# A decoder layer on one core: where three inner values of a feed-forward half are worked out

## The chip, the cores and the metric

The kernel runs on one core of a Trainium2 chip. The metric is the device time of one execution in microseconds, and smaller is better. The profile that is read here is of one execution; the time before is the median of three runs.

## The reference

A decoder layer in float32 on four batches of 1024 tokens with 512 features. Three residual blocks follow each other, each behind a layer norm: a gated self-attention with 16 heads of 32, a cross-attention to a context of 384 features, and a feed-forward block, which is the one that matters here.

```python
x = x + attn(layernorm(x))                      # 16 heads, softmax with gates
x = x + xattn(layernorm(x), ctx)                # 16 heads, softmax(q k / sqrt(32)) v, then Wo + bo
# feed-forward: M = 64, INNER = 16
s = layernorm(x) @ Win + bin_                   # 64 values a token
h = relu(s[..., None] * W1 + b1)                # 16 inner values of each
g = einsum('btmh,mh->btm', h, W2) + b2          # summed over the 16
x = x + g @ Wout + bout
```

## The kernel before, in words

The work is cut into eight units, `order` (L336): for each of the two attentions (`ph`) the four batches. Unit 0 to 3 are the self-attention, unit 4 to 7 the cross-attention, followed by the feed-forward block of its batch. A unit has two halves of 512 queries, and a half has 32 steps: four groups of four heads (`g`), eight blocks of 128 keys (`kt`) each.

A step (`step`, L684) is written out in this order. TensorE makes the scores of one group and one block into two PSUM buffers (L574). ScalarE takes the exponential of each of the two (L579, tile `e`), which frees the buffer for the scores of the next step. VectorE adds the exponentials up (L585, L587, tile `es`). TensorE then multiplies the exponentials of the step before with the values (L601, tile `av`), and, in the self-attention and in the last unit, adds half of the heads up itself (L609, tile `sm`). In units 4 to 6 VectorE adds up both exponentials of a step, in unit 7 only one, save in the very last group. A step after a group has ended, its sums are made by TensorE (L631) and copied out by ScalarE (L618, L620, L632); they travel over DRAM, come back as reciprocals, and VectorE multiplies the group's output with them (L681).

Between the steps stands the other work: projections of the next unit, and the output projection, the norm and the feed-forward block of the half before. `beside(u, hf)` (L962) writes it out as a list of parts, each with a load; `run` (L930) hands them out to the 32 steps in proportion to their loads, in the order of the list. A part with load 0 takes no share and goes with its neighbour; `pause` is a part with a load and no work. `weave(light, items)` (L918) spreads the parts of `light` evenly among those of `items`.

The feed-forward block of a half lies in `post` (L728). `inputs` makes the 64 values a token (L841) and ScalarE copies them out (L280, tile `sT`). Then `hidden(h)` (L853), for h from 0 to 16, takes one of the 16 inner values and adds up the one before:

```python
if h < INNER:
    hid = p2.tile([P, 2 * P], F32, tag="hid", name="hid")
    nc.scalar.activation(hid, res["s"], AF.Relu, ...)                     # L858
if h == 1:
    nc.vector.tensor_scalar(res["g"], res["hid"], ...)                    # L862
elif h > 1:
    nc.vector.scalar_tensor_tensor(res["g"], res["hid"], ..., res["g"])   # L864
```

The tile `hid` has two buffers, so ScalarE's inner value h waits until VectorE has taken value h - 2. All these parts have load 0. `outputs` ends the block (L875, L881). What `some(half, k)` (L957) takes off, the first k of the 17 parts, is laid out with the half of attention in which `inputs` stands; the rest is kept in `held` and laid out with the next half. So the block of unit 6's first half, `post(6, 0)`, begins beside the second half of unit 6 (`beside(6, 1)`, L1008 to L1015) and ends beside the first half of unit 7 (`beside(7, 0)`, L966 to L977). In this last list the first six parts that are left go with a pause of ten, and all others with the 16 parts of the output projection of unit 6's second half (L972).

[...] SyncE issues the transfers.

Of the kernel before, what the change touches and what calls it, by code (L numbers as in the profile page):

```python
# [63 lines left out]
def moderate_path(tc: tile.TileContext, a: dict, out: bass.AP, flag: bass.AP):  # L64
    nc = tc.nc
    x = a["x"]
    with ExitStack() as st:
# [130 lines left out]
        def rotate(c):  # L198
            def f():
                pw = bank()  # L200
                columns(pw, rot[:, c, :], raw[0][:, c, :], start=True, stop=True)
                nc.vector.tensor_copy(raw[0][:, c, :], pw)
                if c == NC - 1:
                    nc.sync.dma_start(wout_d, raw[0])
            return [(1, f)]
# [40 lines left out]
        def load_networks(k):  # L246
            r = slice(k * M, (k + 1) * M)
            nc.gpsimd.dma_start(wout[r, :], a["ffn_Wout"])
            nc.gpsimd.dma_start(fb[r, :], a["ffb"])
            for c in range(NF):  # L250
                for w in range(3):
                    nc.gpsimd.dma_start(
                        units[k * M + c * per : k * M + (c + 1) * per, w, :],
                        a["units"].rearrange("(m h) w c -> c w m h", h=INNER)[c, w],
                    )
# [81 lines left out]
        n = len(order)  # L337
# [580 lines left out]
        def weave(light, items):  # L918

            first, second = sum(light, []), sum(items, [])  # L920
            out, done = [], 0
            for n, f in enumerate(first):
                upto = (2 * n + 1) * len(second) // (2 * len(first))
                out += second[done:upto] + [f]
                done = upto
            return [out + second[done:]]
# [14 lines left out]
        def pause(load):  # L941
            return [[(1, None)] * load]

        n = len(order)
        pres = [pre(u) for u in range(n)]

        def one(f):
            return [[(0, f)]]
# [4 lines left out]
        def ahead(u, what):  # L953

            return one(lambda: pres[u]["load"](what))

        def some(half, k):  # L957

            h, half["h"] = half["h"][:k], half["h"][k:]
            return h  # L960

        def beside(u, hf):  # L962

            last = post(u, 0) if hf else post(u - 1, 1) if u else None
            end = lambda items: weave(held[0]["h"], items) + (lambda o: o[0:1] + pause(1) + o[1:] + pause(1))(held.pop()["out"]) if held else items
            if u + 1 == n:  # L966
                h, out = held[0]["h"], last["wo"] + last["load"]
                k = min(len(h), 6)
                if hf:
                    ending.append(post(u, 1))  # L970
                    out += ending[0]["wo"]
                out += pause(2) + weave(h[0:k], pause(10)) + weave(h[k:], last["o"]) + held.pop()["out"]  # L972
                out += (ending[0]["load"] if hf else []) + weave(last["ln"], pause(5)) + last["xT"]
                out += weave(last["b"], pause(8))
                out += weave(last["tr"], pause(3)) + last["s"] + weave(some(last, 8), pause(14))
                held.append(last)
                return out  # L977
            p = pres[u + 1]
            x, ln, xT, tr, k, q, v = (p[i] for i in ("x", "ln", "xT", "tr", "k", "q", "v"))
            next_ = pres[u + 2] if u + 2 < B else None  # L980
            if u + 1 < B:
                if hf == 0:
                    if last:
                        out = x[1] + last["wo"] + last["load"] + ahead(u + 1, "v") + k[0][0:1] + p["g"][0] + k[0][1:] + p["gt"][0]
                        out += weave(ln[1], last["o"]) + xT[1] + weave(last["ln"], v[0][0:2])
                    else:
                        out = one(fold_bv) + x[1] + k[0][0:1] + [rotate(c) for c in range(NC)]
                        out += ahead(u + 1, "v") + p["g"][0] + k[0][1:2] + [[(4, fold_bv)]] + weave(ln[1], k[0][2:])
                        out += p["gt"][0] + v[0][0:1] + xT[1] + v[0][1:2]
                    return out + tr[1] + v[0][2:3] + p["g"][1] + v[0][3:] + p["gt"][1]  # L990
                if not next_:
                    out = k[1] + ahead(u + 1, "q") + last["wo"] + last["load"] + v[1] + ahead(u + 2, "k") + last["o"]
                    return out + weave(last["ln"], q[0][0:2]) + q[0][2:] + pres[u + 2]["ctx"][0] + q[1]
                out = next_["x"][0] + k[1][0:2] + last["wo"] + last["load"] + weave(next_["ln"][0], k[1][2:] + v[1])
                out += ahead(u + 1, "q") + ahead(u + 2, "k") + last["o"]
                out += weave(last["ln"], q[0][0:2]) + q[0][2:] + next_["xT"][0] + q[1][0:3] + next_["tr"][0] + q[1][3:]
                if u == 1:
                    out = one(lambda: load_networks(0)) + out + one(lambda: load_networks(1)) + one(fold_bin)
                return out
            if hf == 0:  # L1000
                out = ahead(u + 1, "v") + last["wo"] + p["ctx"][1] + end(k[0] + v[0][0:2]) + last["load"]
                out += last["o"] + weave(last["ln"], v[0][2:])
                if "s" in last:
                    out += last["xT"] + k[1][0:2] + weave(last["tr"], k[1][2:3]) + [k[1][3][0:2]] + last["s"]
                    held.append(last)
                    return out + xT[0] + weave(last["b"] + some(last, 5), [k[1][3][2:]] + v[1][0:2]) + tr[0]
                return out + k[1] + xT[0] + v[1][0:2] + tr[0]
            out = ahead(u + 1, "q") + last["wo"] + end(v[1][2:] + q[0][0:3]) + xT[1]  # L1008
            out += (ahead(u + 2, "k") if u + 2 < n else []) + last["load"] + last["o"] + tr[1]
            out += weave(last["ln"], q[0][3:] + q[1][0:1])  # L1010
            out += pres[u + 2]["ctx"][0] if u + 2 < n else []
            if "s" in last:
                out += last["xT"] + weave(last["b"], q[1][1:2]) + weave(last["tr"], q[1][2:3]) + [q[1][3][0:2]] + last["s"]
                held.append(last)
                return out + weave(some(last, 3), [q[1][3][2:]])  # L1015
            return out + q[1][1:]

        p = pres[0]
# [16 lines left out]
        for u in range(n):  # L1035
            if u == 0:
                crossing.append(True)
            for hf in range(2):
                run(attention(u, hf), beside(u, hf))
# [679 lines left out]
```

## Time and profile before

| | us |
|---|---|
| median of three runs | 2210.0 (2209.04 to 2211.79) |
| the profiled execution, its own time | 2212.44 |
| its span, first to last instruction | 2210.6 |
| TensorE busy in the span | 2174.1 (98%) |
| VectorE busy | 1562.2 (71%) |
| ScalarE busy | 1238.5 (56%) |
| one exponential (L579) | 1.022 |
| one sum of exponentials (L587) | 1.227 |
| one inner value (L858) | 0.605 |
| one product with the second weights (L864) | 0.481 |

The span is what the trace covers. PE is TensorE's matmuls, PEld its weight loads, DVE is VectorE, ACT is ScalarE, SPq is SyncE's queue. A line of the timeline gives start, length, engine, line of the kernel, operation and tiles (written, then read); "x16" says that so many instructions are put together, and the brackets give the idle time of the engine before it and who ended it. The granted clock of TensorE is 1.00 at full speed.

### The profile page before, as it was taken

Reading aid. Unit: us, or ns where it says so; the run is one execution under the profiler, and the core shown is the slowest. Engines: PE = TensorE matmul, PEld = TensorE weight load, DVE = VectorE, ACT = ScalarE, POOL = GpSimd, SP = SyncE. Lnnn points to the kernel's source line nnn. Section 1 sums busy time; section 2 is a strip of 40 time slices with the busy share of each in tenths; the row PEclk is TensorE's granted clock in tenths of the full one; section 3 lists DMA queues with packets and bytes.
Section 4 is the critical chain, followed back from the end, with each engine's and each line's share of the span. In section 5 each row is a group of like instructions: output and inputs, shape, how many; then the busy total and the mean of one; then the engine's idle time right before and its main releaser. Section 6 shows DMA issues by size and latency. Waiting matters only on the chain.

```text
span 2210.6 us, 52746 instructions
## 1 busy us (share of the span) xinstructions
PE 2174.1 (98%) x22598; PEld 547.7 (25%) x22598; DVE 1562.2 (71%) x2526; ACT 1238.5 (56%) x1489; POOL 82.0 (4%) x118
## 2 busy tenths in 40 slices
PE   8999999999999999999999999999999999999995
PEld 3322222222222222222222222222222222222222
DVE  4478675796757957577686666877787777856476
ACT  0155545555455554555556565676757566667673
POOL 1000000030300000000000000000000000000000
PEclk9999999999999999999999999999999999999998
DMA  4412123032230211211232132312233142303031
GB/s 142 132 56 63 55 98 106 24 88 66 100 106 25 85 66 55 79 37 51 60 89 89 45 87 64 101 60 65 58 98 87 60 97 64 88 12 117 21 88 40
DMA packets 153304, 161.70 MB, mean 73 GB/s; under 512 B 46202, under 2 KB 91898, under 8 KB 151908
## 3 DMA queue, kind: packets, MB, share of 16 engines
q1 hardware_dynamic: 149068, 156.14, 24.4%
q8 instruction: 179, 2.93, 0.6%
q0 software_dynamic: 2144, 0.98, 0.3%
q10 hardware_dynamic: 1848, 1.12, 0.2%
q14 instruction: 65, 0.53, 0.1%
HBM read 115.40 MB, written 42.74 MB: 72 GB/s over the span
## 4 chain that ended last, share of the span: by engine, by line
PE 92%; DVE 3%; issue 2%; DMA 2%; ACT 2%; SPq 0%; DVEq 0%; ACTq 0%
PE f L87 35%; PE s L574 24%; PE av L601 21%; PE sm L609 6%; PE sm L631 3%; DVE es L587 1%; ACT e L579 1%; PE f L875 1%; DMA xn<-rows_d 1%; DVE g L864 1%; PE f L841 1%; DMA rows_d<-r 0%; PE f L325 0%; PE f L471 0%; PE f L1025 0%
## 5 line engine op out<-in xcount | busy, mean ns | idle before, releaser
L579 ACT ACTIVATE e<-s 128x1024 f32<-128x1024 f32 x1024 | 993.7, 1022 | 713.2 <-PE s L574 518.0
L587 DVE TENSOR_TENSOR es<-es,e 128x1024 f32<-128x1024 f32 x534 | 642.3, 1227 | 255.8 <-ACT e L579 253.5
L574 PE MATMUL s<-q,k 32*64 32x512 f32 x8192 | 608.7, 614 | 4.5 <-ACT e L579 2.9
L601 PE MATMUL av<-e,v 128*32 128x512 f32 x4096 | 551.1, 604 | 0.0
L87 PE MATMUL f<-xT,w 128*32 128x512 f32 x2816 | 333.7, 592 | 0.6 <-PE f L87 0.6
L595 DVE SCALAR_TENSOR_TENSOR eg<-e,sw,eg 128x512 f32<-128x512 f32 x448 | 318.6, 747 | 2.3
L585 DVE TENSOR_TENSOR es<-e 128x1024 f32<-128x1024 f32 x89 | 106.7, 1222 | 221.0 <-ACT e L579 187.8
L574 PEld LDWEIGHTS s<-q,k 32*64 32x64 f32 x8192 | 133.1, 130 | 449.4 <-ACT e L579 243.3
L87 PE MATMUL f<-w,q 128*32 128x512 f32 x1984 | 240.5, 592 | 0.7 <-DVE q L720 0.7
L601 PEld LDWEIGHTS av<-e,v 128*32 128x32 f32 x4096 | 88.1, 108 | 404.6 <-issue 401.4
L87 PEld LDWEIGHTS f<-xT,w 128*32 128x32 f32 x2816 | 92.1, 110 | 211.3 <-issue 204.4
L609 PE MATMUL sm<-e,sw 128*2 128x512 f32 x1024 | 133.3, 592 | 0.0
L87 PE MATMUL f<-w,xT 128*32 128x512 f32 x896 | 106.0, 592 | 0.6 <-DVE q L284 0.6
L87 PEld LDWEIGHTS f<-w,q 128*32 128x32 f32 x1984 | 65.5, 110 | 150.0 <-issue 142.3
L858 ACT ACTIVATE hid<-sT,units 128x256 f32<-128x256 f32 x128 | 76.7, 605 | 31.1 <-DVE g L864 24.5
L87 PE MATMUL f<-w,ctxT 128*32 128x512 f32 x768 | 92.6, 592 | 0.0
L87 PE MATMUL f<-ctxT,w 128*32 128x512 f32 x768 | 92.3, 592 | 0.0
L778 POOL TENSOR_TENSOR r<-res,bo_bc 128x512 f32<-128x512 f32 x32 | 40.9, 1278 | 1040.5 <-DVE res L770 702.7
L631 PE MATMUL sm<-es,ones 128*1 128x512 f32 x348 | 65.8, 601 | 0.0
L864 DVE SCALAR_TENSOR_TENSOR g<-hid,units,g 128x256 f32<-128x256 f32 x120 | 57.7, 481 | 11.3 <-ACT hid L858 5.8
L770 DVE TENSOR_TENSOR res<-f,res 128x512 f32<-128x512 f32 x62 | 42.5, 686 | 17.9 <-PE f L87 8.9
L681 DVE TENSOR_TENSOR q<-both,recb 128x512 f32<-128x512 f32 x63 | 43.3, 687 | 7.5 <-DMA recb<-rec_d 7.5
(258 smaller groups left out, 1037.2 us busy)
## 6 DMA issues: line engine op xcount, KB each, us to landing
recb<-rec_d SPq DMA_DIRECT2D x252, 64.0 KB
xT<-rows_d SPq DMA_DIRECT2D x60, 256.0 KB
rows_d<-r SPq DMA_DIRECT2D x60, 256.0 KB
w<-in_xattn_Wo SPq DMA_DIRECT2D x9, 1024.0 KB
w<-wout_d SPq DMA_DIRECT2D x8, 1024.0 KB
res<-in_x SPq DMA_DIRECT2D x32, 256.0 KB
x1b_d<-r SPq DMA_DIRECT2D x32, 256.0 KB
res<-x1b_d SPq DMA_DIRECT2D x32, 256.0 KB
```

Of the source, the lines that this page charges most:

```text
L87: nc.tensor.matmul(to[r], lhsT=lhsT[:, j, :] if len(lhsT.shape) == 3 else lhsT[:, r], rhs=rhs, **flags)
L574: nc.tensor.matmul(s[m : m + 64, j, :], lhsT=k[r, g, kt * P + m : kt * P + m + 64], rhs=q[r, g, :], start=True, stop=True,)
L579: nc.scalar.activation(e, s, AF.Exp, scale=SCALE)
L585: nc.vector.tensor_tensor(me["es"][i], me["e", 0][i], es[i], ALU.add)
L587: nc.vector.tensor_tensor(me["es"][i], me["es"][i], es[i], ALU.add)
L595: nc.vector.scalar_tensor_tensor(eg, es[0][:, h, :], gate(kt), eg, ALU.mult, ALU.add)
L601: nc.tensor.matmul(av[r, :], lhsT=me["v"][:, kt, HG * g + h, :], rhs=es[h // 2][:, h % 2, :], start=(kt == 0), stop=(kt == NT - 1),)
L609: nc.tensor.matmul(sm[j * DH : j * DH + sums, :], lhsT=me["sw"][:, t, HG * g + 2 + h, :] if ph == 0 else ones, rhs=me["e", t][1][:, h, :], ...
L631: nc.tensor.matmul(sm[j * DH : j * DH + 1, :], lhsT=ones, rhs=e, start=True, stop=True)
L681: nc.vector.tensor_tensor(me["q", hf][:, g, :], both[:, 0, :], all_, ALU.mult)
L858: nc.scalar.activation(hid, res["s"], AF.Relu, bias=units[:, 1, h : h + 1], scale=units[:, 0, h : h + 1])
L864: nc.vector.scalar_tensor_tensor(res["g"], res["hid"], units[:, 2, h - 1 : h], res["g"], ALU.mult, ALU.add)
```

## The change

For unit 6 alone, no inner value of its first half's feed-forward block is laid out beside its own second half; all 17 parts go with the first half of unit 7. Units 4 and 5 keep their three.

```diff
@@ beside(u, hf) @@
             if "s" in last:
                 out += last["xT"] + weave(last["b"], q[1][1:2]) + weave(last["tr"], q[1][2:3]) + [q[1][3][0:2]] + last["s"]
                 held.append(last)
-                return out + weave(some(last, 3), [q[1][3][2:]])
+                return out + (weave(some(last, 3), [q[1][3][2:]]) if u + 2 < n else [q[1][3][2:]])
             return out + q[1][1:]
```

In the list of unit 7's first half, 17 parts instead of 14 are now spread in the same places: six with the pause of ten, eleven instead of eight with the 16 parts of the output projection. The loads of both lists are what they were, so every part with a load stays in its step.

## The prediction

> **What bounds the kernel now.** First the page: the busy times and the row of granted clock.
>
> ```profile
> span 2210.6 us, 52746 instructions
> ...
> PE 2174.1 (98%) x22598; PEld 547.7 (25%) x22598; DVE 1562.2 (71%) x2526; ACT 1238.5 (56%) x1489; POOL 82.0 (4%) x118
> ```
>
> TensorE is idle for only 36.5 us of 2210.6. Work moved between ScalarE and VectorE can therefore matter only where it makes TensorE wait or slows its clock. So I asked for TensorE's waits on ScalarE: apart from the end of the program there is one large one, 2.17 us at 1931, the join of unit 6 and unit 7, which is where the moved instructions stand. The timeline of TensorE there (start, length, work; in brackets the idle time before it and what ended it):
>
> ```profile
> 1929.01 1.11 PE L574 MATMUL s<-q,k 32*64 32x512 f32 x16
> 1930.06 1.07 PE L601 MATMUL av<-e,v 128*32 128x512 f32 x8
> 1933.30 2.89 PE L574 MATMUL s<-q,k 32*64 32x512 f32 x16 [2.17 <-ACT e L579]
> 1936.12 1.89 PE L631 MATMUL sm<-es,ones 128*1 128x512 f32 x8
> 1937.78 1.93 PE L601 MATMUL av<-e,v 128*32 128x512 f32 x8
> 1939.64 1.23 PE L574 MATMUL s<-q,k 32*64 32x512 f32 x16
> ```
>
> The reader is to see the hole, and that the same av work takes 1.07 us before it and 1.93 us after it. The busy times by stretch say why (the column after POOL is TensorE's granted clock):
>
> ```profile
> 1931.10:1933.10 2.00, 0.02 (x4) 0.00 (x0) 0.97 (x2) 1.94 (x3) 0.00 (x0) 1.00 0.02 4
> 1933.20:1939.90 6.70, 6.60 (x40) 1.36 (x48) 1.62 (x2) 4.95 (x8) 0.00 (x0) 0.50 0.00 1
> 1940.00:1946.00 6.00, 6.00 (x68) 1.34 (x56) 3.11 (x6) 4.61 (x6) 0.00 (x0) 1.00 0.03 3
> ```
>
> The hole is followed by 6.8 us at half clock. What made the hole stands in ScalarE's timeline, with VectorE's at the same time below it:
>
> ```profile
> 1928.24 0.60 ACT L858 ACTIVATE hid<-sT,units 128x256 f32<-128x256 f32 x1
> 1931.16 0.60 ACT L858 ACTIVATE hid<-sT,units 128x256 f32<-128x256 f32 x1 [2.32 <-DVE g L862]
> 1931.66 0.67 ACT L282 ACTIVATE q<-f,bqk 128x512 f32<-128x512 f32 x1
> 1932.23 1.92 ACT L579 ACTIVATE e<-s 128x1024 f32<-128x1024 f32 x2
> ...
> 1928.38 2.36 DVE L587 TENSOR_TENSOR es<-es,e 128x1024 f32<-128x1024 f32 x2
> 1930.65 0.41 DVE L862 TENSOR_SCALAR g<-hid,units,fb 128x256 f32<-128x256 f32 x1
> ```
>
> The third inner value (1931.16) needs the buffer of the first, which is free only after the product at L862; that stands on VectorE behind the sums of exponentials. Behind the inner value ScalarE's queue holds the evacuation of q and the pair of exponentials whose scores TensorE began at 1929.01; TensorE's next scores need those two PSUM buffers. The chain of what ended last runs through just these instructions here.
>
> [...] the exponentials stand for 2 us behind an instruction they do not need. [...] The half-clock stretch runs from 1933.13 to 1939.96[...].
>
> **The change, part by part.** Nothing is added or removed: for one unit, three ScalarE activations of 0.60 us, one L862 of 0.41 us and, counting the whole accumulation, the later L864 products of 0.48 us are issued later. In the built order TensorE, Pool and SyncE have the same sequence; no DMA and no projection moves.
>
> (1) The join. Without inner values there, ScalarE takes the q evacuation 0.14 us after the following scores start, as it did at 1917.32 after scores at 1917.18: 1929.15 to 1929.84. The pair of exponentials started 1.16 us after its scores in that step (1918.34), so at 1930.17, not 1932.23. Its first ends after 1.02 us, at 1931.19; TensorE followed 0.06 us after such an end (1933.24, 1933.30), so scores at 1931.25. TensorE's own av ends at 1931.12: the hole shrinks from 2.17 to 0.13 us, **2.04 us** gained. The second half of these scores waits for the second exponential (1932.11), so it starts at 1932.17 and takes 1.01 us as at 2011.32. Then the four sum matmuls (0.86), av (0.98): next scores at 1935.02, where the trace has 1939.64. That is **4.62 us** in all, so 2.58 us of it is the half clock. (6.83 us at half rate would be 3.4; the rest was time that this stretch waits for exponentials at any clock.)
>
> (2) The first steps of unit 7. Inner values 0 to 4 stand just where 3 to 7 stood, one in each of steps 0 to 4: nothing changes. In step 1 the sum L585 now precedes L862 and waits for the sum matmuls, done by about 1934.1; inner value 2 asks for L862's result a step later. No wait.
>
> (3) Steps with two. The loads of unit 7's list are unchanged, so 11 rather than 8 inner values spread over the 8 steps with output projection: steps 5, 8 and 10 hold two. The worst is step 5, in times of before:
>
> ```profile
> 1951.65 0.60 ACT L858 ACTIVATE hid<-sT,units 128x256 f32<-128x256 f32 x1
> 1952.03 0.68 DVE L681 TENSOR_TENSOR q<-both,recb 128x512 f32<-128x512 f32 x1
> 1952.15 1.94 ACT L579 ACTIVATE e<-s 128x1024 f32<-128x1024 f32 x2
> 1952.63 0.48 DVE L864 SCALAR_TENSOR_TENSOR g<-hid,units,g 128x256 f32<-128x256 f32 x1
> ...
> 1956.41 1.11 PE L574 MATMUL s<-q,k 32*64 32x512 f32 x16
> ```
>
> The second inner value needs the product that ends at 1953.11, so it runs 1953.2 to 1953.8 and the exponentials start near 1953.7, 1.55 us late. The scores that need their buffers start at 1956.41; the first exponential then ends at 1954.7 and the second at 1955.6 against 1956.9. The 1.90 us of projection in between is the cover: **0**, with 1.3 us left; uncovered it would cost 1.55. In step 8 the second one runs about 1964.65 to 1965.25, before the next exponentials are ready (1965.93); in step 10 about 1973.3 to 1973.9 against 1975.12. **0** for both.
>
> (4) After that the order is the same again, and work that hangs on TensorE moves up. Unknown is the end: shorter holes there (1.92 us before 2168.85) also bring a half-clock stretch, 2168.65 to 2175.48. [...] about 2.6 us gained at best if it vanishes; at worst the same lost again if another appears. I take 0, as the longest hole there looks alike.
>
> Sum: -2.04 - 2.58 + 0 = -4.62, a span of 2206.0. The profiled execution took 2212.44 (1.84 around its span), so it would take 2207.8. The timed runs are shorter (2209.04 to 2211.79)[...]: some may lack a half-clock stretch. Against the median I take the same 4.6, 2210.0 to 2205.4.
>
> **The rivals.** *Only the wait goes*: in the typical run the half clock never followed the hole[...]. Speaks for it: the profiled run is the slowest of all shown, by 2.4 over the median. [...] Gain 2.04, so 2208.0.
>
> *Nothing changes*: the exponentials were late for another reason, such as the q evacuation ahead of them, or the joins of the earlier units hide such a wait. At 1681.85 the same wait (2.06 us) cost TensorE only 0.20 us, because a 1.90 us projection stood there; at 1931 the list is at a pause, and nothing stands there. So unlikely: 2210.
>
> *Slower*: the doubled inner values make a loop through in-order queues. VectorE's product for the earlier one stands behind the residual work of a projection (0.69 + 0.69 + 0.18 us, L770 to L775), which waits for TensorE; so TensorE, VectorE and ScalarE wait for each other in steps 8 and 10. It decides once a doubled step delays the second exponential by over 1.3 us beyond what I worked out. If two steps each make a hole like the present one with its half clock (2 x 4.62), less the 4.62 gained, the time is 2214.6. Against it: in step 10 the product behind the projection is done by 1971.4, and the next inner value cannot start before 1972.34 anyway.
>
> *More than the sum*: the half-clock stretch at the end goes too, 2202.8.
>
> **How the numbers follow.** Wait and half clock both go 0.56; only the wait 0.17; nothing 0.08; slower 0.11; more than the sum 0.08. A measurement of this kernel tells 0.2%, 4.4 us, from no change, so the likeliest case sits close to the bound: I count 0.40 of its 0.56 as faster and 0.16 as within. Faster 0.40 + 0.08 = 0.48; within 0.2% 0.16 + 0.17 + 0.08 = 0.41; slower 0.11. The time is that of the likeliest, 2205.4, its own range 2203.5 to 2207.5. The range must take in the case with the wait alone and most of no change, down to the end's gain: 2202.5 to 2210.3, which leaves out the slower case and the rest of the best one.
>
> **What would show it.** Right: no idle time above 0.3 us on TensorE near 1931, scores at about 1931.25 and 1935.0, full clock there, exponentials of step 6 about 1.5 us later within their step and still no hole before the next scores. Wrong: a hole at steps 6 to 11 ended by an exponential behind L858; a new half-clock stretch in unit 7; or the hole at 1931 still there, ended by L282 or a VectorE sum.

## The result, and the profile after

The changed kernel takes 2206.78 us (median of 20 runs, 2206.08 to 2207.93), the kernel before 2210.69 us (20 runs, 2208.11 to 2213.24). The ratio is 0.9981, 95% interval 0.9975 to 0.9987: it is 3.9 us, or 0.19%, faster. That falls just short of the 0.2%, 4.4 us, from which the prediction counted a kernel as faster, and the interval takes in both sides of this bound. It also scatters less: its runs lie within 1.9 us of each other, those of the kernel before within 5.1. The profiled execution of the changed kernel took 2206.22 us. Its page:

```profile
span 2204.3 us, 52747 instructions
...
PE 2169.4 (98%) x22598; PEld 547.9 (25%) x22598; DVE 1563.1 (71%) x2526; ACT 1238.1 (56%) x1489; POOL 81.7 (4%) x118
```

All the work is still there: PE, PEld, DVE, ACT and POOL have as many instructions as before. TensorE's timeline at the join of unit 6 and unit 7:

```profile
1928.60 1.11 PE L574 MATMUL s<-q,k 32*64 32x512 f32 x16
1929.64 1.06 PE L601 MATMUL av<-e,v 128*32 128x512 f32 x8
1930.83 2.00 PE L574 MATMUL s<-q,k 32*64 32x512 f32 x16
1932.76 1.04 PE L631 MATMUL sm<-es,ones 128*1 128x512 f32 x8
1933.62 1.04 PE L601 MATMUL av<-e,v 128*32 128x512 f32 x8
1934.59 1.11 PE L574 MATMUL s<-q,k 32*64 32x512 f32 x16
```

The brackets with 2.17 us of idle time are gone, and the sum and av matmuls take 1.04 us each, where they took 1.89 and 1.93. From the first scores of this list to the last it is 5.99 us; before it was 10.63. On ScalarE the evacuation and the exponentials follow each other, with no inner value ahead of them or between them:

```profile
1928.74 0.69 ACT L282 ACTIVATE q<-f,bqk 128x512 f32<-128x512 f32 x1 [0.80 <-PE f L87]
1929.75 1.94 ACT L579 ACTIVATE e<-s 128x1024 f32<-128x1024 f32 x2 [0.33 <-PE s L574]
```

The exponentials now wait for the scores, not for an inner value. The busy times by stretch, with the granted clock after POOL, show full clock throughout:

```profile
1930.80:1934.50 3.70, 3.67 (x32) 0.77 (x32) 0.61 (x1) 3.70 (x6) 0.00 (x0) 1.00 0.01 2
1934.60:1945.00 10.40, 10.40 (x112) 2.33 (x112) 6.07 (x11) 8.36 (x12) 0.00 (x0) 1.00 0.13 29
```

Step 5 of unit 7, the one with two inner values that the prediction worked through, in the timeline of all engines:

```profile
1947.46 1.07 DVE L864 SCALAR_TENSOR_TENSOR g<-hid,units,g 128x256 f32<-128x256 f32 x2
...
1948.03 0.60 ACT L858 ACTIVATE hid<-sT,units 128x256 f32<-128x256 f32 x1 [0.95 <-DVE g L864]
1948.54 1.92 ACT L579 ACTIVATE e<-s 128x1024 f32<-128x1024 f32 x2
...
1951.24 1.11 PE L574 MATMUL s<-q,k 32*64 32x512 f32 x16
```

The second value does wait for VectorE, and the exponentials start at 1948.54. That is 3.61 us earlier than in the kernel before (1952.15), where the scores around them are 5.2 us earlier (1956.41 to 1951.24): they are late by 1.6 us within their step. TensorE does not wait for it.

The two profiled spans differ by 6.3 us, more than the medians. Of this, 0.4 us was there before the join; 4.6 us come from the join; 0.3 us from the stretch between it and the end of the program; and the end gives 0.9 us. There the granted clock was 0.50 for 3.41 us in this execution (2164.04 to 2167.45) and for 6.83 in that of before (2168.65 to 2175.48), so the 32 matmuls of the output projection took 4.28 us instead of 5.62; the rest of the end, the last matmuls above all, took some 0.5 us more.

### The profile page after: what moved, and what is told of

Its sections match the earlier page's. It is cut to its first block, busy times and chain, and to the rows that moved or that the text cites. A ratio compares the mean times of both kernels' runs of the same rounds, so it can differ in the third digit from the quotient of the medians.

```text
span 2204.3 us, 52747 instructions
## 1 busy us (share of the span) xinstructions
PE 2169.4 (98%) x22598; PEld 547.9 (25%) x22598; DVE 1563.1 (71%) x2526; ACT 1238.1 (56%) x1489; POOL 81.7 (4%) x118
## 4 chain that ended last, share of the span: by engine, by line
PE 93%; DVE 2%; ACT 1%; issue 1%; DMA 1%; SPq 0%; DVEq 0%; ACTq 0%
PE f L87 36%; PE s L574 25%; PE av L601 21%; PE sm L609 6%; PE sm L631 3%; ACT e L579 1%; PE f L875 1%; DMA w<-in_attn_Wo 1%; PE f L841 1%; DVE es L587 1%; DVE g L864 1%; DMA sum_d<-both 0%; PE f L471 0%; PE s L87 0%; PE f L325 0%
```

## The experiments

Four questions stood open: is it the third inner value's wait for its buffer that makes the hole; how much of the loss is the wait and how much the half clock; why do the runs gain less than the profile; and what did the doubled steps cost.

**A buffer of its own.** The kernel before, its instructions in the same order on every engine; only one tile lies elsewhere.

```diff
-hid = p2.tile([P, 2 * P], F32, tag="hid", name="hid")
+hid = p2.tile([P, 2 * P], F32, tag="hid", name="hid") if (u, hf, h) != (n - 2, 0, 2) else p2.tile([P, D], F32, tag="r2", name="hid")[:, 0 : 2 * P]
```

> The kernel before, with every instruction in its place; only the third inner value of unit 6 gets a buffer of its own, so it no longer waits for the product at L862. Theory (that one wait makes the hole, the hole makes the half clock): TensorE's hole at the join shrinks from 2.17 to below 0.3 us, no half-clock stretch follows, and the time is that of the changed kernel, about 2206.8, 3.9 us below the kernel before. Rival (three inner values and the evacuation of q are simply too much work ahead of the exponentials): three inner values still stand there, the exponentials are late by at least 0.6 us, and at most half of the gain comes, 2208.7 or more. Rival (it is where the values stand later that matters): no change, 2210.7.

Measured: 2206.42 us (21 runs) against 2210.08 of the kernel before on the same chip, ratio 0.9984 (0.9977 to 0.9991). ScalarE's timeline at the join:

```profile
1927.49 1.09 ACT L858 ACTIVATE hid<-sT,units 128x256 f32<-128x256 f32 x2
1928.47 0.68 ACT L282 ACTIVATE q<-f,bqk 128x512 f32<-128x512 f32 x1
1929.42 1.94 ACT L579 ACTIVATE e<-s 128x1024 f32<-128x1024 f32 x2 [0.27 <-PE s L574]
```

All three values stand where they stood, two of them back to back, and ScalarE still waits for the scores before the exponentials. TensorE has no hole there. So the amount of work ahead of the exponentials was never too large, and nothing is gained by where the values stand later: one wait for one buffer was the cause. The gain of the change is had without moving anything.

**Two early instead of three.** `some(last, 3)` becomes `some(last, 2)` for unit 6.

> The kernel before with two instead of three inner values of unit 6 laid out early; the other fifteen go with unit 7. Theory (only the third one waits): no hole above 0.3 us at the join, time as the changed kernel, 2206.8 within 0.7. Rival (each of the three costs a share): about a third of the gain, near 2209.4.

Measured: 2206.19 us against 2210.08, ratio 0.9982 (0.9975 to 0.9989), as low as the changed kernel (2206.78). The first two cost nothing; the third took it all.

**The hole filled.** The kernel before, and two matmuls that nobody reads in the pause at the start of unit 7:

```diff
+def busy():
+    for _ in range(2):
+        nc.tensor.matmul(sm, lhsT=ident, rhs=bo_bc, start=True, stop=True)
-out += pause(2) + weave(h[0:k], pause(10)) + ...
+out += (pause(2) if hf else [[(1, busy), (1, None)]]) + weave(h[0:k], pause(10)) + ...
```

> The kernel before with two matmuls added that fill TensorE's hole at the join with 1.7 us of work that nobody reads (a product of the unit matrix into the sums' PSUM tile before its next use). The exponentials are as late as before, so the wait of 2.04 us stays; only the idleness goes. Theory (part of the loss is the half clock that idleness brings): full clock after the join, the following scores still about 4.2 us after those before them, time near 2208.7 (the changed kernel and 2.0), and the runs lie within 2 us of each other as those of the changed kernel do, not over 5 us as those of the kernel before. Rival (the half clock costs the typical run nothing, all of the loss is the wait): 2210.7, no change.

Measured: 2208.45 us (13 runs, 2207.49 to 2209.51) against 2210.08. TensorE's timeline, L960 being the added matmuls:

```profile
1927.99 1.11 PE L574 MATMUL s<-q,k 32*64 32x512 f32 x16
...
1930.03 1.98 PE L960 MATMUL sm<-bo_bc,ident 128*128 128x512 f32 x4
1932.27 2.00 PE L574 MATMUL s<-q,k 32*64 32x512 f32 x16 [0.26 <-ACT e L579]
1934.20 1.04 PE L631 MATMUL sm<-es,ones 128*1 128x512 f32 x8
1935.06 1.04 PE L601 MATMUL av<-e,v 128*32 128x512 f32 x8
1936.03 1.11 PE L574 MATMUL s<-q,k 32*64 32x512 f32 x16
```

The exponentials are as late as ever (these scores end a wait for them), but what follows runs at full rate: 1.04 us each for the sum and av matmuls, against 1.89 and 1.93. It divides the loss: from the kernel before to this one 1.6 us, which is the half clock in a typical run, and from this one to the version with a buffer of its own 2.0 us, which is the wait. From scores to scores over the join (1927.99 to 1936.03) it is 8.04 us here, 2.05 more than in the changed kernel, so the trace gives the wait the same size. The interval of the first part, 0.9984 to 1.0001, just touches no change; that the runs lie within 2.0 us of each other, and those of the kernel before within 5.0, speaks for it.

**The kernel before, profiled twice more.**

> The kernel before once more, for one profile. Theory [...]: the hole at the join is again 2.1 to 2.2 us, but the half-clock stretch after it begins elsewhere, or has another length, or is missing; the scores after next come 8.6 us (no half clock) to 11.5 us after those before the hole, 10.6 in the profile shown. Rival (hole and half clock are the same in every run, the runs differ elsewhere): the stretch begins 2.0 us into the hole, lasts 6.8 us, and the distance is 10.6 within 0.1.

> The kernel before a third time, for one profile; the same is expected as of the one before it[...].

The hole was 2.18 and 2.16 us. The first of these executions took 2210.35 us; TensorE's timeline in it, then the busy times after the half clock began:

```profile
1928.04 1.11 PE L574 MATMUL s<-q,k 32*64 32x512 f32 x16
...
1937.66 1.17 PE L574 MATMUL s<-q,k 32*64 32x512 f32 x16
```

```profile
1934.50:1937.80 3.30, 3.30 (x24) 0.58 (x24) 1.62 (x2) 2.58 (x4) 0.00 (x0) 0.50 0.00 0
1937.90:1944.00 6.10, 6.10 (x68) 1.39 (x64) 3.16 (x7) 4.66 (x6) 0.00 (x0) 1.00 0.03 3
```

Half clock from 1934.5 to 1937.8 and full clock from 1937.9, so some 3.3 us of it instead of 6.83 (the first scores after the hole, at 1932.33, still took 2.00 us and not 2.89), and 9.62 us between these scores instead of 10.63. The other execution took 2212.51 us; its granted clock was 0.50 from 1932.8 to 1939.5, some 6.7 us, and 1.00 from 1939.6, the distance 10.62. So the same hole costs a different amount from run to run, and the execution shown before was one of the dear ones. Against the 8.04 us of the filled hole, the half clock cost 1.58 us in the execution with 3.3 us of it and 2.59 and 2.58 in those with 6.8 and 6.7; the 1.6 us that the medians give the half clock is what the short stretch costs. How the runs divide between no half clock, the short stretch and the long one is not known. The distance over the join makes up 1.0 of the 2.2 us between the times of these two executions; the rest of it lies elsewhere. A run with no half clock at all was not caught in a profile.

**Nine with the pause.** The changed kernel with `k = min(len(h), 9)` for unit 7's first half: the doubled steps come where no projection stands.

> The changed kernel, but nine instead of six inner values go with the pause of ten, so that the steps with two of them lie where no projection covers them (steps 1, 3 and 4 of unit 7), and none lies among the projections. Theory (a second value delays the next exponentials by 0.4 to 1.5 us and only the projection hid that): TensorE waits after these steps, 1.5 to 4 us in all, time 2208.3 to 2210.8[...]. Rival (two values in a step cost nothing anywhere, since ScalarE is busy half of the time only): as the changed kernel, 2206.8 within 0.7.

Measured: 2206.69 us, ratio to before 0.9986 (0.9979 to 0.9992), the same as the changed kernel. Against that one's trace the exponentials of steps 4 and 5 are up to 1 us later, and TensorE shows one hole of 0.26 us; its scores are set back by 0.5 us in all. ScalarE at one of these steps, then TensorE at the hole:

```profile
1945.34 0.60 ACT L858 ACTIVATE hid<-sT,units 128x256 f32<-128x256 f32 x1 [0.35 <-DVE g L864]
1945.85 1.92 ACT L579 ACTIVATE e<-s 128x1024 f32<-128x1024 f32 x2
...
1946.90 2.00 PE L574 MATMUL s<-q,k 32*64 32x512 f32 x16 [0.26 <-ACT e L579]
```

The expected 1.5 us and more did not come. The second values waited only 0.35 us for VectorE in these steps, so the delay itself was smaller than the 1.6 us of step 5 in the changed kernel; what 1.6 us would cost where no projection stands, this run does not show.

**No early values at any join.** The changed kernel, and units 4 and 5 without their three as well.

```diff
-return out + (weave(some(last, 3), [q[1][3][2:]]) if u + 2 < n else [q[1][3][2:]])
+return out + [q[1][3][2:]]
```

> The changed kernel with the same edit for units 4 and 5 too: no inner value of theirs is laid out beside the half before. Theory (their joins have a projection of 1.9 us under the same wait, so nothing is to be won): as the changed kernel, 2206.5 within 0.7; TensorE's idle time at 1683, 0.2 to 0.33 us, goes or halves. Rival (each join with three early values costs something that the trace does not show as idle time): 2 to 4 us faster than the changed kernel, 2203 to 2204.5.

Measured: 2208.22 us (13 runs) against 2210.46, ratio 0.9990 (0.9981 to 0.9998): slower than the changed kernel by some 1.5 us, which neither theory said. The idle time at 1683 is gone, and against the scores ahead of them those behind the two joins are 0.5 and 1.3 us earlier. But in the steps after them more inner values are doubled. Two such steps in ScalarE's timeline, then VectorE between them, then TensorE:

```profile
1706.32 0.61 ACT L858 ACTIVATE hid<-sT,units 128x256 f32<-128x256 f32 x1 [1.51 <-DVE g L864]
1706.83 1.91 ACT L579 ACTIVATE e<-s 128x1024 f32<-128x1024 f32 x2
...
1710.71 0.60 ACT L858 ACTIVATE hid<-sT,units 128x256 f32<-128x256 f32 x1 [1.49 <-DVE g L864]
1711.22 1.92 ACT L579 ACTIVATE e<-s 128x1024 f32<-128x1024 f32 x2
...
1707.86 2.36 DVE L587 TENSOR_TENSOR es<-es,e 128x1024 f32<-128x1024 f32 x2 [1.05 <-ACT e L579]
1710.14 1.07 DVE L864 SCALAR_TENSOR_TENSOR g<-hid,units,g 128x256 f32<-128x256 f32 x2
...
1707.88 2.00 PE L574 MATMUL s<-q,k 32*64 32x512 f32 x16 [0.28 <-ACT e L579]
```

Here a second value waits 1.51 and 1.49 us, where it waited 0.35 in the experiment before: in these units VectorE adds up both exponentials of a step ahead of the product that frees the buffer. The exponentials come late, VectorE's sums wait for them (1.05 us), and so the next product is late too. TensorE has new holes of 0.28 and 0.32 us, at 1707.6 behind the exponentials of 1706.83 and at 1716.4 behind a later pair. Measured on the scores, steps 7 to 10 lose 1.9 us in unit 5 and as much in unit 6, which is more than the joins gain. It is a loop of the kind that the slower rival described, with the sums of exponentials where that had the residual work. In the changed kernel a second value also waits in unit 6, up to 1.85 us, and no hole follows; there at most two doubled steps stand in a row, here four. That their row makes the holes is read from the two traces and not tested by itself.

**The holes of the end filled.** The changed kernel, with two matmuls that nobody reads between the two output parts of the end and ten before the last inner values (`busy` as above, with their number given, into the tile `av`):

```diff
-go(o[1], o[3], *o[4:6], *sum(held[0]["out"], []), ln[0], ...
+outs = sum(held[0]["out"], [])
+go(o[1], o[3], *o[4:6], outs[0], (0, lambda: busy(2)), outs[1], ln[0], ...
...
+busy(10)
 go(*h[4:], *sum(tail["out"], []))
```

> The changed kernel with matmuls that nobody reads in the two long holes of the program's end: two (1.7 us) in the hole of 1.92 us between the two output parts, ten (8.6 us) in the last one of 10.4 us. The waits stay, the idleness goes. Theory (holes cost half clock at the end as at the join): full clock to the end, the 32 output projection matmuls after the first hole and the last eight each at full rate, 2 to 4 us faster than the changed kernel, 2202.8 to 2204.8. Rival (the end waits for VectorE and for transfers, not for TensorE's rate): within 0.7 of the changed kernel.

Measured: 2203.32 us (6 runs, 2202.89 to 2204.27) against 2210.46, ratio 0.9968 (0.9956 to 0.9981): faster than both kernels, by some 3.3 us over the changed one (3.5 by the medians, 3.2 by the distance of each to the kernel before beside it). TensorE's timeline of the end, first in the changed kernel, then in this one:

```profile
2163.50 2.67 PE L875 MATMUL f<-wout,g 64*128 64x512 f32 x4 [1.92 <-DVE res L881]
2166.10 4.28 PE L87 MATMUL s<-w,q 128*32 128x512 f32 x32
...
2193.14 3.79 PE L875 MATMUL s<-wout,g 64*128 64x512 f32 x8 [10.41 <-DVE g L864]
```

```profile
2163.95 1.72 PE L875 MATMUL f<-wout,g 64*128 64x512 f32 x4
2165.60 3.64 PE L87 MATMUL s<-w,q 128*32 128x512 f32 x32
...
2192.00 1.99 PE L875 MATMUL s<-wout,g 64*128 64x512 f32 x8 [1.63 <-DVE g L864]
```

The 32 matmuls take 3.64 us instead of 4.28 and the last eight 1.99 instead of 3.79. VectorE's work that they wait for is as late as before; only the clock is other: 1.00 from 2163.0 to 2172.0 and 0.83 on the mean from 2190.0 to 2201.0, where the changed kernel has 0.50 from 2164.1 to 2167.4 and from 2188.0 to 2204.0.

## Why the prediction was right or wrong

*The cause* was right as put: the third inner value waits for a buffer behind VectorE's sums, and the exponentials wait behind it. A separate buffer takes the whole loss away.

*Step 1, the join.* From scores to scores over the join 6.01 us were forecast and 5.99 measured, so 4.64 us gained in the trace against 4.62. The wait was forecast at 2.04 us and is 2.0 by the filled hole.

*Its second term was mis-sized for the typical run.* The 2.58 us of half clock held for the profiled execution, which had 6.83 us of it. The median run loses 1.6 us. The prediction said that some runs may lack a half-clock stretch, set the case of no half clock beside the main one, and yet took the full 4.6 us against the median. That is large enough for the 0.7 us between 4.62 forecast and 3.9 measured; the other half of the 1.4 us between 2205.4 and 2206.78 is the median of before, 2210.0 from three runs and 2210.69 from twenty. Of the forecast's two likely cases, the time lies between the one with both and the one with the wait alone. The lean towards "faster", 0.48 against 0.41 for within 0.2%, rested on this term too: with 3.9 us for 4.62 the change came out on the other side of the bound, by less than the interval can tell.

*Step 2*, no new wait in the first steps of unit 7: right. *Step 3*, the doubled steps: right, the exponentials 1.6 us late within step 5 against 1.55, and no hole. How much of this the projection covers is not shown: with doubled values among the pauses 0.5 us were lost, but there they delayed the exponentials by 1.0 us at most. *Step 4*, the end: the stretch there was 3.41 us instead of 6.83 in the profiled execution. Whether that is the change's doing is not shown. What it costs in the typical run was not measured by itself.

*The rivals.* No change and slower are refuted for this change; a loop like that of the slower one cost 1.9 us a unit in the run with no early values, where VectorE does two sums a step. *Only the wait goes* is refuted by the time itself: even the near end of the interval, 0.9987, is a gain of 2.9 us, and the wait is 2.0.

## What to carry to other kernels

Where two engines feed each other, ask of every small instruction whose buffer it needs, not how long it takes: here the exponentials stood behind an inner value that waited 2.32 us for its buffer, and 0.6 us of work held TensorE for 2 us. Price a hole in TensorE's work with the half clock after it, and profile more than one execution for that part, because it differs from one to the next: 1.58 and 2.58 us for the same hole here. A buffer more can give what moving work gives (2206.42 us here, and 2206.78 by the move); matmuls that nobody reads, where the wait must stay, can give the part of the clock (1.6 us at the join).

## What the runs showed of the hardware that was not expected

At the join a hole of 2.16 to 2.18 us in TensorE's work was followed by a granted clock of 0.50 in all three profiles of the kernel before, for 6.83 and some 6.7 and 3.3 us. Without the hole the clock was 1.00 from 1928.6 to 1945.0 in the changed kernel; with it filled, the sum and av matmuls took the same 1.04 us as there.

How long a hole has to be is not shown, and its length alone does not decide. The hole of 1.92 us at the end stands in both kernels. In the profile of before the half clock began at 2168.65, 0.20 us before the hole's end, and lasted 6.83 us; in that of the changed kernel it began at 2164.04, 0.54 us after the hole's end, and lasted 3.41 us. With the holes of the end filled, one of 1.63 us was left, from 2190.37 to 2192.00 (rough, since the profile models the ends of matmuls), and the eight matmuls right behind it took 1.99 us, against 3.79 at a granted clock of 0.50.

In these two profiles the stretches between two changes of the clock lasted 6.83, 228.69, 6.83, 17.07, 10.24 and 3.41 us (before) and 3.41 and 20.48 us (changed): each is a whole multiple of 3.413 us, to 0.01 us. Why is not shown.

Matmuls that nobody reads, at two places of the end, were worth some 3.3 us (2203.32 against 2206.78), nearly as much as the change.
